# Layer 0 of a four-layer kernel: another order on TensorE, another split of one product, and a gate one step earlier

## The chip, the cores and the metric

The kernel runs on one core of one Trainium2 chip. The metric is the device time of one execution in microseconds, the median of several runs. Lower is better. A profile of one further execution shows where that time lies.

The core has five engines that the text names as the profile does: PE is TensorE (matrix products), PEld its weight loads, DVE is VectorE, ACT is ScalarE, POOL is GpSimd, and SP is SyncE, which issues the transfers. Each works through its own queue in order and waits where an operand or a buffer is not there yet.

## The reference, cut to what matters

The input has two images of 128 channels and 64 x 64 places. Four layers follow one another. Only layer 0 is touched: four selective scans over each image (row order, row order reversed, column order, column order reversed), fused and added to the input.

```python
xz = x @ W_in.T
xh, z = jnp.split(xz, 2, axis=-1)
...
xc = lax.conv_general_dilated(xc, conv_w, (1,), 'VALID', ..., feature_group_count=d_inner)
xc = xc + conv_b[None, :, None]
xh = jax.nn.silu(xc).transpose(0, 2, 1)
x_dbl = xh @ W_xp.T
dt = x_dbl[..., :dt_rank]
Bm = x_dbl[..., dt_rank:dt_rank + N]
Cm = x_dbl[..., dt_rank + N:]
dt = jax.nn.softplus(dt @ W_dt.T + b_dt)
A = -jnp.exp(A_log)
dA = jnp.exp(dt[..., None] * A)
dBu = dt[..., None] * Bm[:, :, None, :] * xh[..., None]

def step(h, inp):
    dA_t, dBu_t = inp
    h = dA_t * h + dBu_t
    return (h, h)
...
y = jnp.einsum('lbdn,bln->bld', hs, Cm)
y = y + xh * Dp
y = y * jax.nn.silu(z)
return y @ W_out.T
```

There are 256 inner channels with 16 states each, so 4096 scans of 4096 places for each order and image. Layer 1 and 2 are attentions, layer 3 is another scan.

## The kernel before, in words

Layer 0 is cut into 64 chunks: 2 images, 2 orders, forward and reversed, and 8 pieces of 512 places. Each chunk has 16 steps. A step handles two blocks of 128 rows (a row is one channel with one state), so the tiles are 128 x 1024. `gq` (line 154) says which states (`g`) and channels (`q`) step `u` has.

For step `u` the work is this. `s_dbu` (L336, GpSimd) makes dt x u x B. `s_da` (L349, ScalarE) makes exp(dt A) in two halves, into one of two PSUM buffers. `s_fix` (L361, L364, ScalarE) adds the state of the chunk before to the first place. `s_scan` (L380, VectorE) runs the recurrence. `s_hst` (L385, ScalarE) saves the last state. `s_hc` multiplies the scan's result by C: on VectorE (L392) with C spread over the rows by TensorE in PSUM, or on GpSimd (L390) with C brought by a transfer. Which steps go to GpSimd is `POOL_HC`. `s_pc` (L369, TensorE) makes that spread for a pair of steps; it has two PSUM buffers. `s_y` (L403, TensorE) sums the products over the states into the one PSUM buffer `y`. `y0` (L396) opens that buffer with the skip term. `yg_` (L410, VectorE) multiplies by the gate, `po_x` and `po` (L420, L425, TensorE) add the input to the projection, and `xo` (L430, L432, ScalarE) writes the image back. The buffers are few: three for `dbu`, three for `h`, four for `hc`, one for `y`, and one for `misc`, the PSUM tile that all other products of TensorE share in turn.

While a chunk `c` runs, pieces of its neighbours run between its steps: the end of the chunk before (`old`), the input work of the next (`new`) and of the one after (`nxt`), and in 12 chunks the normalisation of a later piece of the image. The dictionaries `M`, `A`, `V`, `G` say in which step TensorE, ScalarE, VectorE and GpSimd take such a piece. The pieces that the prediction uses are `pd` (L273, TensorE: dt, B, C before the bias), `xd_` (L278, ScalarE: with the bias), `pt` (L293, TensorE: the dt projection), `abs_`, `e_exp`, `e_ln` (L300, L303, L306, ScalarE: the softplus), `dt_` (L312, VectorE), `dtu_` (L320, GpSimd), `px` and `x_` (L238, L243), `pz` and `z_` (L247, L253). `pd` of the next chunk but one stands in step 15, and `xd_` of that same chunk in step 0 of the following chunk.

The order is written out by hand, under a manual schedule: the order in which the program calls these methods in a step is the order in each engine's queue. In a step it is: `s_dbu` of two steps ahead, the scan, a piece of VectorE, the product of the step before, a piece of GpSimd; then on ScalarE `s_da` and `s_fix` of the next step, the state, and ScalarE's pieces; then on TensorE the spread of C in odd steps, `y0`, the sums, and TensorE's piece; then the gate and the issues of transfers. The sums of a pair come two steps after a product on VectorE and three after one on GpSimd (`pairs`).

Of the kernel before, what the change touches and what calls it, by code (L numbers as in the profile page):

```python
# [16 lines left out]
T = 512  # L17
NCH = L // T
NS = 16
POOL_HC = (1, 5, 9, 11, 14)  # L20
GROUPS_C = (0, 2, 1, 3)
NHC, NH, NDBU = 4, 3, 3
ND = 73
# [33 lines left out]
def conv_seq_kernel(ctx: ExitStack, tc: tile.TileContext, a: dict, out: bass.AP):  # L57
    nc = tc.nc
    mm = nc.tensor.matmul
# [4 lines left out]
    def gt(shape, name, pool=None, **kw):  # L64
        return (pool or gp).tile(shape, F32, tag=name, name=name, **kw)
# [28 lines left out]
    with ExitStack() as c0:  # L94
# [6 lines left out]
        def misc(shape=(P, T)):  # L101
            return ps.tile(list(shape), F32, tag="misc", name="misc")
# [24 lines left out]
        wof = gt([P, 2, 4, P], "wof", wp)  # L127
# [88 lines left out]
        class Chunk:  # L216
# [170 lines left out]
            def s_hc(self, u):  # L387
                t = self.hc[u] = wt("hc", NHC)
                if u in POOL_HC:
                    nc.gpsimd.tensor_mul(t, self.h[u], _bc(self.cs[gq(u)[0]], 1, [P, 2, T]))  # L390
# [18 lines left out]
                    self.yg = wt("dt", 1)  # L409
                nc.vector.tensor_mul(self.yg[:, i, :], self.sz[:, i, :], self.y[i])  # L410

            def po_x(self):
                self.pp = p = misc()
                if self.order:
                    xo = x[:, self.b, :].rearrange("p (h w) -> p w h", w=W)
                    xo = xo[:, self.ci * 8 : self.ci * 8 + 8, :]
                    p = p.rearrange("p (w h) -> p w h", h=H)
                else:
                    xo = x[:, self.b, self.t0 : self.t0 + T]
                mm(p, lhsT=ident, rhs=xo, start=True, stop=False, skip_group_check=True)  # L420
                self.xo_ = xo, p

            def po(self):
                for i in range(2):
                    mm(self.pp, lhsT=wof[:, i, 2 * self.order + self.rev, :], rhs=self.yg[:, i, :],  # L425
                       start=False, stop=(i == 1), skip_group_check=True)

            def xo(self):
# [17 lines left out]
        for u in range(0, 16, 2):  # L446
            pairs.setdefault(max(m + (3 if m in POOL_HC else 2) for m in (u, u + 1)), []).append(u)

        with tc.manual_schedule():
            def norm(j):  # L450
                n = Norm0(0, j)
                for f in (n.center, n.sub, n.square, n.var, n.keep, n.ln, n.exp, n.rows, n.scale,
                          n.mul, n.affine):
                    f()

            for j in range(3):
                norm(j)
            c, c1 = chunks[:2]
            for i in range(2):
                c.px(i)  # L460
                c.x_(i)
            c.xsilu()
            c.pd()
            c.xd_()
            for i in range(2):
                c.pt(i)
                c.abs_(i)
            c.e_exp()
            c.e_ln()
            for i in range(2):  # L470
                c.pt(i)
                c.dt_(i)
                c.dtu_(i)
            c.spread("dts", 0)
            c.states(0, 0)
            c.spread("dus", 0)
            for g in range(1, 4):
                c.states(0, g)
            for g in GROUPS_C:
                c.states(1, g)  # L480
            c.spread("dts", 1)
            c.spread("dus", 1)
            for i in range(2):
                c.pz(i)
                c.z_(i)
            c.s_pc(0)
            c.s_dbu(0)
            c.s_dbu(1)
            c.s_da(0)
            c.s_fix(0)  # L490
            norm(3)
            for i in range(2):
                c1.px(i)
                c1.x_(i)
            c1.xsilu()
            c1.pd()
            old = None
            for k, c in enumerate(chunks):
                new, nxt = (chunks[k + i] if k + i < nk else None for i in (1, 2))
                ln, lp = norms.get(k), norms.get(k - 1)  # L500

                def at(u):
                    return (c, u) if 0 <= u < 16 else ((old, u + 16) if u < 0 else (new, u - 16))

                A, V, M, G = {}, {}, {}, {}
                if old is not None:
                    M[2], M[3], A[4] = old.po_x, old.po, (old.xo,)
                if c.rev:  # L510
                    A[4] = (*A[4], c.zload)
                else:
                    A[8] = (c.zsilu,)
                if new is not None:
                    A[0] = (new.xd_,)
                    M[0], A[1] = lambda: new.pt(0), (lambda: new.abs_(0),)
                    M[1], A[2] = lambda: new.pt(1), (lambda: new.abs_(1), new.e_exp)
                    A[3] = (new.e_ln,)
                    M[4], V[5] = lambda: new.pt(0), lambda: new.dt_(0)
                    M[5], V[6] = lambda: new.pt(1), lambda: new.dt_(1)  # L520
                    G[7], G[8] = lambda: new.dtu_(0), lambda: new.dtu_(1)
                    if not new.rev:
                        M[6], A[7] = lambda: new.pz(0), (lambda: new.z_(0),)
                        M[13], A[14] = lambda: new.pz(1), (lambda: new.z_(1),)
                if nxt is not None:
                    M[8], A[9] = lambda: nxt.px(0), (lambda: nxt.x_(0),)
                    M[10], A[12] = lambda: nxt.px(1), (lambda: nxt.x_(1),)
                    A[13] = (nxt.xsilu,)
                    M[15] = nxt.pd
                if lp is not None:  # L530
                    A[3] = (*A[3], lp.ln, lp.exp)
                    A[6] = (lp.rows,)
                    M[7], V[8] = lp.scale, lp.mul
                    A[10] = (lp.affine,)
                if ln is not None:
                    M[12], V[13] = ln.center, ln.sub
                    A[14] = (*A.get(14, ()), ln.square)
                    M[14], A[15] = ln.var, (ln.keep,)
                if k in turns:
                    A[11] = (lambda: turn(turns[k]),)  # L540

                for s in range(16):
                    (c1, u1), (c2, u2), (cp, up) = at(s + 1), at(s + 2), at(s - 1)

                    if c2 is not None:
                        c2.s_dbu(u2)
                    c.s_scan(s)
                    if s in V:
                        V[s]()
                    if cp is not None:  # L550
                        cp.s_hc(up)
                    if s in G:
                        G[s]()

                    if c1 is not None:
                        c1.s_da(u1)
                        c1.s_fix(u1)
                    if cp is not None:
                        cp.s_hst(up)
                    for f in A.get(s, ()):  # L560
                        f()

                    if s % 2 and s < 15:
                        c.s_pc(s + 1)
                    elif s == 15 and new is not None:
                        new.s_pc(0)
                    if s in (4, 11):
                        c.y0(s // 11)
                    for cy, e in ((c, s), (old, s + 16)):
                        for u in pairs.get(e, ()) if cy is not None else ():  # L570
                            cy.s_y(u)
                            cy.s_y(u + 1)
                    if s in M:
                        M[s]()

                    if s == 2 and old is not None:
                        old.yg_(1)
                    if s == 10:
                        c.yg_(0)

                    if new is not None:
                        if s in (7, 14):
                            new.spread("dts", s // 14)
                        if s in (9, 13):
                            new.spread("dus", s // 13)
                        if s in (8, 10, 12, 14):
                            new.states(0, s // 2 - 4)
                        if s in (11, 12, 13, 15):
                            new.states(1, GROUPS_C[{11: 0, 12: 1, 13: 2, 15: 3}[s]])
                old = c  # L590
            c.s_hc(15)
            for e in (16, 17):
                for u in pairs.get(e, ()):
                    c.s_y(u)
                    c.s_y(u + 1)
            c.yg_(1)
            c.po_x()
            c.po()
            c.xo()

# [11 lines left out]
    with ExitStack() as c1:  # L612
# [296 lines left out]
        for n, j in enumerate(jobs):  # L909
# [10 lines left out]
            if jobs[n - 1].layer == 1:  # L920
                for ci in range(NCH):
                    c = Conv(jobs[n - 1].b, ci)
# [62 lines left out]
    with ExitStack() as c3:  # L985
# [276 lines left out]
        with tc.manual_schedule():  # L1262
            c = chunks[0]
# [13 lines left out]
            for s in range(-1, len(steps) + 3):  # L1277
# [3 lines left out]
                old = chunks[ci - 1] if ci > 0 else None  # L1281
# [209 lines left out]
```

## Time and profile before

| | us |
|---|---|
| median of 3 runs | 6928.74 |
| lowest and highest run | 6912.35, 6931.16 |
| the profiled execution's own time | 6921.35 |
| its span, first to last instruction | 6919.6 |
| layer 0 in it, from the first scan to the end of its last pieces | 108 to 3588 |
| granted clock of TensorE, whole span | 0.863 |

The page gives the busy time of each engine over the whole span: PE 6036.7 (87%), DVE 5525.2 (80%), POOL 5366.3 (78%), ACT 4467.5 (65%). Slices of the page are 173 us each; layer 0 fills the first 20 and a part of the 21st. In a timeline row the first number is the start, the second the time, then engine, line, operation, the tile written and the tiles read; brackets hold the idle time before the row and what ended it. In the waits the columns are the total, how often, and the longest.

### The profile page before, as it was taken

Reading aid. Unit: us, or ns where it says so; the run is one execution under the profiler, and the core shown is the slowest. Engines: PE = TensorE matmul, PEld = TensorE weight load, DVE = VectorE, ACT = ScalarE, POOL = GpSimd, SP = SyncE. Lnnn points to the kernel's source line nnn. Section 1 sums busy time; section 2 is a strip of 40 time slices with the busy share of each in tenths; the row PEclk is TensorE's granted clock in tenths of the full one; section 3 lists DMA queues with packets and bytes.
Section 4 is the critical chain, followed back from the end, with each engine's and each line's share of the span. In section 5 each row is a group of like instructions: output and inputs, shape, how many; then the busy total and the mean of one; then the engine's idle time right before and its main releaser. Section 6 shows DMA issues by size and latency. Waiting matters only on the chain. (4 is left out here: it accounts for less than half of the span.)

```text
span 6919.6 us, 67264 instructions
## 1 busy us (share of the span) xinstructions
PE 6036.7 (87%) x20656; PEld 2806.4 (41%) x20656; DVE 5525.2 (80%) x4494; ACT 4467.5 (65%) x7688; POOL 5366.3 (78%) x2487
## 2 busy tenths in 40 slices
PE   6888888888888888888868999999999997988888
PEld 1222222222222222222217887788788884222222
DVE  3899999999999999999975665566566675887777
ACT  4887778877788777887755665455456554434342
POOL 3899999899999999999975665555556666777776
PEclk8777788787777777777779999999999998889888
DMA  3555565556555655656540000000000001222222
GB/s 111 135 147 148 145 153 139 138 148 152 138 152 149 153 145 145 154 148 151 141 136 7 3 5 1 1 1 1 1 1 13 1 1 54 69 75 75 86 75 67
DMA packets 352652, 616.51 MB, mean 89 GB/s; under 512 B 72473, under 2 KB 74786, under 8 KB 351906
## 3 DMA queue, kind: packets, MB, share of 16 engines
q1 hardware_dynamic: 351552, 610.44, 34.1%
q8 instruction: 162, 2.65, 0.2%
q14 instruction: 200, 1.64, 0.1%
q10 hardware_dynamic: 738, 1.78, 0.1%
HBM read 496.45 MB, written 115.47 MB: 88 GB/s over the span
## 5 line engine op out<-in xcount | busy, mean ns | idle before, releaser
L336 POOL TENSOR_TENSOR dbu<-dus,bs 128x1024 f32<-128x1024 f32 x1024 | 2401.8, 2365 | 216.9 <-DVE h L380 192.6
L380 DVE TENSOR_TENSOR_SCAN h<-da,hst,dbu 128x1024 f32<-128x1024 f32 x896 | 2092.6, 2343 | 120.6 <-ACT dbu L364 120.1
L349 ACT ACTIVATE da<-dts,aneg 128x512 f32<-128x512 f32 (+1 forms) x2048 | 1410.8, 689 | 412.9 <-DVE h L380 373.2
L833 POOL TENSOR_TENSOR sum<-sum,sc 128x1024 f32<-128x1024 f32 x384 | 906.8, 2361 | 495.2 <-ACT sc L828 491.5
L795 ACT COPY sc<-s 128x512 f32<-128x512 f32 x1024 | 597.9, 585 | 867.8 <-PE s L790 753.6
L790 PE MATMUL s<-q,k 128*128 128x256 f32 x4096 | 1058.0, 382 | 11.6 <-ACT q L776 8.4
L802 DVE TENSOR_TENSOR mx<-mx,s 128x512 f32<-128x512 f32 x896 | 610.1, 681 | 569.6 <-ACT sc L795 568.5
L845 PE MATMUL av<-sc,v 128*128 128x256 f32 x4096 | 1049.7, 379 | 2.3 <-ACT sc L828 2.3
L369 PE MATMUL pc<-xd,sel 16*128 16x512 f32 x1024 | 723.1, 792 | 241.4 <-DVE hc L392 241.1
L392 DVE TENSOR_TENSOR hc<-h,pc 128x1024 f32<-128x1024 f32 x704 | 843.2, 1198 | 0.1
L790 PEld LDWEIGHTS s<-q,k 128*128 128x128 f32 x4096 | 781.2, 192 | 146.2 <-issue 36.6
L845 PEld LDWEIGHTS av<-sc,v 128*128 128x128 f32 x4096 | 769.1, 190 | 103.1 <-ACT sc L828 3.7
L403 PE MATMUL y<-hc,cst 128*32 128x512 f32 x4096 | 725.2, 711 | 60.5 <-POOL hc L390 57.7
L390 POOL TENSOR_TENSOR hc<-h,cs 128x1024 f32<-128x1024 f32 x320 | 757.0, 2366 | 1.3 <-issue 1.3
L1160 POOL TENSOR_TENSOR A<-A,D 128x1024 f32<-128x1024 f32 x224 | 526.8, 2368 | 225.3 <-DVE D L1165 201.4
L825 DVE TENSOR_TENSOR sc<-sc,pm 128x1024 f32<-128x1024 f32 x512 | 620.9, 1214 | 0.9 <-PE pm L821 0.9
L828 ACT ACTIVATE sc<-sc 128x1024 f32<-128x1024 f32 x512 | 541.9, 1059 | 8.6 <-DVE sc L825 8.1
L1153 ACT ACTIVATE A<-dtr,aneg 128x1024 f32<-128x1024 f32 (+1 forms) x256 | 245.8, 1030 | 376.3 <-PE y L1185 369.9
L369 PEld LDWEIGHTS pc<-xd,sel 16*128 16x128 f32 x1024 | 180.7, 219 | 622.1 <-DVE hc L392 271.6
L1171 DVE TENSOR_TENSOR A<-A,q 128x1024 f32<-128x1024 f32 (+1 forms) x256 | 276.8, 1081 | 148.1 <-PE q L1137 147.6
L1137 PE MATMUL q<-xs,lb 32*128 32x512 f32 x896 | 332.2, 713 | 69.5 <-DVE D L1147 64.1
L293 PE MATMUL misc<-xd,w_dt 9*128 9x512 f32 x512 | 304.2, 675 | 63.0 <-ACT xd L278 50.7
(210 smaller groups left out, 8065.0 us busy)
## 6 DMA issues: line engine op xcount, KB each, us to landing
dts<-ddt SPq DMA_DIRECT2D x512, 256.0 KB, 5.2
dus<-ddu SPq DMA_DIRECT2D x512, 256.0 KB, 4.9
bs<-rows SPq DMA_DIRECT2D x1024, 64.0 KB, 4.7
cs<-rows SPq DMA_DIRECT2D x1024, 64.0 KB, 3.2
ddt<-dt SPq DMA_DIRECT2D x128, 256.0 KB, 2.0
ddu<-dtu SPq DMA_DIRECT2D x128, 256.0 KB, 2.3
dtr<-ddt SPq DMA_DIRECT2D x448, 64.0 KB, 1.9
rx<-ddx SPq DMA_DIRECT2D x448, 64.0 KB, 1.9
```

The lines of the kernel that those rows point to most:

```text
L336: nc.gpsimd.tensor_mul(t, self.dus[q], _bc(self.bs[g], 1, [P, 2, T]))
L349: act(t[:, i, sl], self.dts[q][:, i, sl], AF.Exp, scale=an[:, g, 2 * q + i : 2 * q + i + 1])
L369: mm(t, lhsT=sel[32:48, 4 * g : 4 * g + 4, :].rearrange("p n d -> p (n d)"), rhs=self.xd[32:48, :], start=True, stop=True)
L380: nc.vector.tensor_tensor_scan(ho, ai, bi, init, ALU.mult, ALU.add)
L390: nc.gpsimd.tensor_mul(t, self.h[u], _bc(self.cs[gq(u)[0]], 1, [P, 2, T]))
L392: nc.vector.tensor_mul(t, self.h[u], _bc(self.pc[u // 2], 1, [P, 2, T]))
L403: mm(self.y[q // 2][r : r + 32, :], lhsT=sum4, rhs=self.hc[u][:, i, :], start=False, stop=(u % 8 >= 6), skip_group_check=True)
L790: mm(p[:, o, :], lhsT=j.k[m // 8][:, m % 8 * P : m % 8 * P + P], rhs=self.q, start=True, stop=True)
L802: nc.vector.tensor_max(self.mx, self.s[0][:, 0:2, :] if u == 1 else self.mx, self.p[u])
L825: nc.vector.tensor_sub(s, s, _bc(self.pm[:, :], 1, [P, 4, NQ]))
L833: nc.gpsimd.tensor_add(self.sum, self.s[0] if w == 1 else self.sum, self.s[w])
L845: mm(self.av, lhsT=self.job.v[m // 8][:, m % 8, :], rhs=self.s[u // 2][:, m % 4, :], start=(m == 0), stop=(m == 31))
```

## The change

Four things are done, all in layer 0. On TensorE the spread of C (`s_pc`) is called after the sums and the piece of a step, where it was called before them. `POOL_HC` has step 0 in place of step 1, so GpSimd multiplies the result of step 0 by C and VectorE that of step 1; with this the sums of the first pair move from step 4 to step 3. The second half of the gate of the chunk before (`old.yg_(1)`) is called in step 1 and not in step 2, and `y0(0)` in step 3 and not in step 4. `po_x` becomes a part of `po`, and the whole stands in step 2, where before its first product stood in step 2 and the other two in step 3.

```diff
-POOL_HC = (1, 5, 9, 11, 14)
+POOL_HC = (0, 5, 9, 11, 14)
...
-            def po_x(self):
-                self.pp = p = misc()
+            def po(self):
+                p = misc()
...
+                self.xo_ = xo, p
                 mm(p, lhsT=ident, rhs=xo, start=True, stop=False, skip_group_check=True)
-                self.xo_ = xo, p
-
-            def po(self):
+                if self.order:
+                    p = p.rearrange("p w h -> p (w h)")
                 for i in range(2):
-                    mm(self.pp, lhsT=wof[:, i, 2 * self.order + self.rev, :], rhs=self.yg[:, i, :],
+                    mm(p, lhsT=wof[:, i, 2 * self.order + self.rev, :], rhs=self.yg[:, i, :],
                        start=False, stop=(i == 1), skip_group_check=True)
...
-                    M[2], M[3], A[4] = old.po_x, old.po, (old.xo,)
+                    M[2], A[4] = old.po, (old.xo,)
...
-                    if s % 2 and s < 15:
-                        c.s_pc(s + 1)
-                    elif s == 15 and new is not None:
-                        new.s_pc(0)
-                    if s in (4, 11):
+                    if s in (3, 11):
                         c.y0(s // 11)
                     for cy, e in ((c, s), (old, s + 16)):
                         for u in pairs.get(e, ()) if cy is not None else ():
...
                     if s in M:
                         M[s]()
-
-                    if s == 2 and old is not None:
+                    if s % 2 and s < 15:
+                        c.s_pc(s + 1)
+                    elif s == 15 and new is not None:
+                        new.s_pc(0)
+
+                    if s == 1 and old is not None:
                         old.yg_(1)
...
             c.yg_(1)
-            c.po_x()
             c.po()
             c.xo()
```

## The prediction

> **What bounds the kernel now.** I read the page's busy shares and its slices first: PE shows 87%, but layer 0 (the first 20 slices) is where the change lies, and there DVE and POOL stand at 9 in every slice. So I cut the span at the end of the last scan. TensorE's granted clock, in tenths by slice:
>
> ```profile
> PEclk8777788787777777777779999999999998889888
> ```
>
> The first 20 digits lie mostly at 7 and 8. The table by stretches has layer 0 as one row:
>
> ```profile
> 108.00:3588.00 3480.00, 2921.11 (x7785) 785.30 (x7786) 3276.66 (x2007) 2749.36 (x5242) 3270.85 (x1468) 0.78 0.58 145
> ```
>
> The columns are the stretch, its length, then busy time of PE, weight loads, DVE, ACT, POOL, then the granted clock. DVE works 3276.7 of 3480.0 us, POOL 3270.9. Each idles about 205 us, 3.2 us in each of the 64 chunks. The change adds and removes no VectorE or GpSimd work, so it can win only from these 205 us (3.0% of the kernel); it can lose without limit. Who ends the waits:
>
> ```profile
> DVE h L380 <- ACT dbu L364: 120.1, 158, 2.9
> DVE dt L312 <- PE pc L369: 19.5, 34, 1.2
> DVE dt L410 <- issue: 16.0, 16, 1.7
> DVE dt L410 <- PE y L403: 13.2, 13, 1.2
> ACT xd L278 <- PE misc L273: 131.7, 60, 5.1
> ```
>
> Columns: total us, times, longest. VectorE's scan waits mostly for ScalarE's fix of the carried state (L364), which stands behind the whole ScalarE queue; and ScalarE itself stood 131.7 us (2.2 us a chunk) before `xd_`, waiting for TensorE's `pd`. The timeline of one reverse chunk (its first scan starts at 1556.05) shows the link:
>
> ```profile
> 1553.20 2.07 PE L369 MATMUL pc<-xd,sel 16*128 16x512 f32 x2 [2.64 <-DVE hc L392]
> 1555.20 1.94 PE L403 MATMUL y<-hc,cst 128*32 128x512 f32 x8
> 1557.07 3.69 PE L273 MATMUL misc<-xs,m 128*73 128x512 f32 x4
> 1560.80 0.68 ACT L278 ACTIVATE xd<-misc,vec 73x512 f32<-73x512 f32 x1 [2.43 <-PE misc L273]
> 1561.53 0.69 PE L293 MATMUL misc<-xd,w_dt 9*128 9x512 f32 x1 [0.77 <-ACT xd L278]
> 1561.54 0.69 PE L369 MATMUL pc<-xd,sel 16*128 16x512 f32 x1
> 1562.59 1.07 PE L403 MATMUL y<-hc,cst 128*32 128x512 f32 x8
> ...
> 1574.07 2.35 DVE L380 TENSOR_TENSOR_SCAN h<-da,hst,dbu 128x1024 f32<-128x1024 f32 x1 [1.27 <-ACT dbu L364]
> ```
>
> pc, sums and `pd` follow each other at half clock; `xd_` waits 2.43; ScalarE then runs without a gap from 1560.80 until scan(5), which is 1.27 late. In the next chunk the same three ran partly at full clock, `xd_` came 1.9 us sooner after its first scan, and scan(5) did not wait. Chunk lengths differ accordingly:
>
> ```profile
> 1556.05:1610.15 54.10, 45.82 (x127) 12.06 (x120) 51.07 (x32) 41.10 (x82) 51.31 (x24) 0.78 0.59 148
> 1610.15:1661.87 51.72, 41.14 (x114) 10.76 (x116) 50.94 (x33) 41.27 (x82) 50.97 (x24) 0.83 0.60 153
> 2038.62:2093.56 54.94, 47.32 (x126) 12.71 (x122) 51.30 (x32) 46.45 (x90) 51.23 (x24) 0.75 0.57 145
> 1221.29:1279.30 58.01, 49.45 (x135) 14.22 (x134) 52.60 (x34) 48.28 (x98) 51.45 (x24) 0.79 0.55 139
> ```
>
> Rows 1 and 2: reverse chunks (32 of 64, idle about 1.95 us in the mean of the timeline). Row 3: a forward chunk (19, idle 3.1). Row 4: a forward chunk that also normalises (12, idle 5.4). POOL's 51.0 to 51.4 us of work lies close below every length: a chunk cannot get much under 51.5.
>
> **The change, part by part.** In each part I say who gains.
>
> *The spread of C behind sums and pieces.* No instruction is added. In step 15 `pd` no longer stands behind pc: it starts 2.07 us sooner in the row above (1.1 at full clock). `xd_` then starts when ScalarE is ready: after the state copy that ends at 1558.37, or when `pd` ends (1553.20 + 1.94 + 3.69 = 1558.83). So 1558.85 for 1560.80, 1.95 sooner. In normalising chunks (the row of `xd_` at 1285.54 waits 3.95) it is 2.0 sooner, because `misc` is free (L185 ends at 1279.50). In step 9 the sums of 6 and 7 come 1.1 us sooner, and the gate of step 10 (33 us idle in all, 0.9 in a forward chunk) stops waiting. But scan(11) then meets da(11), behind `x_(0)`, which waits for the end of `px(0)`; that did not move. In the forward chunk da(11)'s fix ends 0.4 before the present scan(11), so 0.4 of the 0.9 is kept, and in normalising chunks nothing: there the norm's piece now goes ahead of pc(8), waits for `z_(0)`, and pushes `px(0)` back by about 0.6. What now queues behind pieces: pc(2) behind pt(1), which waits for `abs_`; pc(4) behind the sums of 0 and 1; pc(6) behind pt(1), which waits for VectorE's `dt_(0)`; pc(8) and pc(14) behind norm and z pieces. Their readers on VectorE come one or two steps later (hc(2) some 4 us after pc(2) would end), so I cost these at nothing; without that cover each would cost up to its 1.1 to 2.1 us.
>
> *The gate of the old chunk in step 1, `po` in one piece in step 2.* Same VectorE work (0.67 us), one step sooner. Cost: the sums of 14 and 15 must end by the end of scan(1), 1559.40 + 2.34 = 1561.74; before, they had until scan(2), 3.7 us later. Their chain is `xd_`, pt(0), sums. From `xd_` at 1558.85: 0.68 + 0.05, pt(0) 1.12, sums 1.07, 0.1 to be seen: 1561.9, a stall of 0.15 at full clock. At half clock pt(0) 2.0 and sums 1.94 make it 1563.6, a stall of 1.9. Behind the waiting gate stand scan(2) and hc(1) on VectorE; for scan(2) wait da(4) on ScalarE and dbu(5) on GpSimd. In forward chunks `xd_` can start 2.15 after the first scan: stall 0 to 1.3. In normalising ones it starts 4.2 after: 1.6 to 3.3. I take 0.5, 0.35 and 2.1, near the full-clock end, because in the two reverse chunks the half clock ends between 2.6 and 6.0 us after the first scan, and pt(0) and sums would run from 3.5 on.
>
> [...] The rows show the pair pt(0) and pc at 1561.53 and 1561.54, both done after 1.12 us: [...] Now pc(0) of the new chunk stands ahead of pt(0) and the two start about 0.7 us apart; [...] if they run in turn, pt(0) is up to 2.0 later and the reverse chunk stalls up to 3. No row shows them staggered; [...] from 1553.20 to 1560.76 PE had no gap, and still the half clock lasted until about 1562. By that row the stall is 1.9. My 0.5 lies nearer to the fast chunk.
>
> *GpSimd takes product 0, not 1.* 2.37 us of POOL and 1.20 of DVE each trade one step. POOL runs dbu(2), dbu(3), dbu(4) back to back (7.00 from 1557.81), then hc(1). Now hc(0) stands between dbu(3) and dbu(4): dbu(4) ends at 1567.2 instead of 1564.8. fix(4) on ScalarE, which would come to it at 1566.35, waits 0.8 in reverse chunks; behind it stand the Ln with two table loads and da(5). From fix(4) to scan(5) it is 5.89 (1568.18 to 1574.07), so scan(5) is at 1573.1: 1.0 sooner than in the slow chunk, but 0.55 to 0.85 later than in the fast one. Forward chunks have 1 us more lead on POOL and pay about nothing. hc(0) must free the buffer that scan(3) writes: 0.9 to 1.4 us to spare.
>
> **The sum**, per chunk. Reverse: scan(5) gains 1.0 or loses 0.7 in turn (+0.15), the dt wait (0.86 in slow ones, later `po` no longer in its way) +0.2, stall beyond what the wait at scan(5) hides -0.3: about 0; x32 = 0. Forward: scan(5) is now bound by VectorE alone, 0.6 sooner after the stall, plus 0.4 at scan(11): 1.0; x19 = 19. Normalising: 1.5 at scan(5) with a stall of 1.7, 1.1 with my 2.1, less 0.25 at scan(11): 0.85; x12 = 10. Together 29 us. The other layers, the DMA issues (none is moved) and chunk 0 are left as they are. The profiled execution took 6921.35 us (span 6919.6, 1.75 around it), so 6892; the median of the runs, 6928.74, lies 7.4 higher and gives 6900. I say 6895.
>
> **Rivals.**
> *Everything is hidden* (0.13): stall 0, fix(4) not late. Reverse chunks go to 51.9 (0.9 each), forward gain 1.9, normalising 2.6: 29 + 36 + 31 = 96, so 6830. For it: the fast chunk's 51.72. Against: POOL's own 51.0 to 51.4 leaves no lead there.
> *No difference* (0.18, within 0.3%, 6908 to 6950, which is about what a measurement can tell): half-clock stalls eat the 29 us; 6925.
> *Slower* (0.37): the gate in step 1 stalls because pt(0) runs behind pc(0) at half clock. Stalls 3.0, 2.4, 3.5: reverse +1.9, forward +0.75, normalising +0.35, 61 + 14 + 4 = 79, so 7000; with half the chunks at full clock about 6960. I put it at 6970. It decides from about 0.5 us more stall per chunk than I took (29/63 eats the gain), 0.8 for slower by 0.3%. For it: the clock row of 0.78. Against: the fast chunk's sums ended in time for exactly this gate.
>
> **How the numbers follow.** Likeliest: a small gain, 6895 (own range 6865 to 6915), chance 0.32 that it is over 0.3%, and the part of it that is less goes to "no difference". Faster: 0.32 + 0.13 = 0.45; same 0.18; slower 0.37. Range: 6820 below the full gain's 6830, and 6990 above, near the full stall's 7000; about 0.1 is left outside on each side.
>
> **What would show it.** Right: the wait of `xd_` for `pd` falls from 131.7 to below 60 us; waits of the gate (L410 before) at step 10 vanish and new ones at step 1 stay under 50 us in all; scan waits for L364 fall from 120 to about 70; reverse chunks all near 52.8. ScalarE's fix waits for GpSimd's dbu(4) some 20 to 30 us, where it was 5.2. Wrong: the gate waits for PE more than 100 us, or the granted clock in layer 0 moves by more than 0.02 from 0.78.

## The result

The changed kernel takes 6866.9 us (median of 6 runs, 6855.92 to 6880.17); the kernel before, on the same chip, 6920.51 (median of 6, 6906.10 to 6931.16). The ratio is 0.9924, 95% interval 0.9906 to 0.9941: 54 us or 0.76% faster. The forecast was 6895, with 6865 to 6915 as the range of its likeliest case. The direction was right, but the gain is nearly twice the 29 us of its sum. The runs below show that the move in step 15, where the forecast put most of the gain, pays only together with a part that it counted at nothing, and that two of the other parts cost time.

The profiled executions are 59 us apart: 6921.35 before, 6862.33 after (span 6860.5). Layer 0, from the first scan to the last, went from 3474.8 to 3426.5, which is 48.3. The other 10.8 lie outside that stretch, where the program is the same. Over all kernels below what lies outside took 3429 to 3451 us with nothing changed in it, so I compare layer 0 where I compare traces.

TensorE's granted clock by slice, and layer 0 as one row (stretch, length, then busy time of PE, weight loads, DVE, ACT, POOL, granted clock, DMA share, GB/s):

```profile
PEclk8777777778777777777769999999999998988898
```

```profile
108.00:3540.00 3432.00, 2908.18 (x7782) 804.08 (x7780) 3272.33 (x2006) 2755.18 (x5242) 3268.35 (x1468) 0.77 0.59 147
```

VectorE and GpSimd have the same work as before (3272 and 3268 us); what went is idle time, some 205 us before and 160 now. The mean clock is 0.77 where it was 0.78, so it gave nothing. Some of the waits, by what ended each (total us, times, longest):

```profile
ACT xs L243 <- PE misc L238: 81.1, 43, 4.4
DVE h L380 <- ACT dbu L364: 74.6, 130, 1.4
ACT dbu L364 <- POOL dbu L336: 39.3, 48, 2.2
DVE dt L410 <- PE y L403: 34.9, 34, 1.9
ACT xd L278 <- PE misc L273: 28.8, 22, 2.5
DVE dt L410 <- issue: 22.4, 10, 2.6
```

`xd_`'s wait for `pd` fell from 131.7 to 28.8 us, the scan's wait for the fix (L364) from 120.1 to 74.6. Two waits are new: 34.9 us of the gate for the sums (before 13.2, in another step), and 39.3 us of the fix for GpSimd's `dbu` (before 5.2). The reverse chunk that was shown of before, in the timeline of after (its first scan is at 1541.32):

```profile
1538.47 1.92 PE L403 MATMUL y<-hc,cst 128*32 128x512 f32 x4 [1.45 <-DVE hc L392]
...
1540.33 3.36 PE L273 MATMUL misc<-xs,m 128*73 128x512 f32 x4
...
1543.61 1.12 PE L369 MATMUL pc<-xd,sel 16*128 16x512 f32 x2
1543.72 0.68 ACT L278 ACTIVATE xd<-misc,vec 73x512 f32<-73x512 f32 x1
...
1544.46 1.12 PE L293 MATMUL misc<-xd,w_dt 9*128 9x512 f32 x2
...
1545.51 1.07 PE L403 MATMUL y<-hc,cst 128*32 128x512 f32 x8
...
1546.64 0.69 PE L293 MATMUL misc<-xd,w_dt 9*128 9x512 f32 x1
...
1546.65 0.69 PE L369 MATMUL pc<-xd,sel 16*128 16x512 f32 x1
...
1546.94 0.66 DVE L410 TENSOR_TENSOR dt<-sz,y 128x512 f32<-128x512 f32 x1
...
1552.38 0.39 ACT L364 ACTIVATE dbu<-hst,dbu,df 128x1 f32<-128x1 f32 x1 [0.63 <-POOL dbu L336]
...
1558.28 2.35 DVE L380 TENSOR_TENSOR_SCAN h<-da,hst,dbu 128x1024 f32<-128x1024 f32 x1 [0.56 <-ACT dbu L364]
```

Sums, `pd`, pc is now the order; `xd_` starts 2.40 after the first scan, where it started 4.75 after. pt(0) and the sums follow, and the gate at 1546.94 comes before scan(2). Then the fix of step 4 waits 0.63 for `dbu`, and scan(5), 16.96 after the first scan (18.02 before), still waits 0.56. The same four chunks as before, by stretch:

```profile
1208.53:1266.52 57.99, 49.21 (x138) 14.86 (x137) 52.39 (x34) 48.24 (x98) 51.37 (x24) 0.76 0.54 135
1541.32:1593.39 52.07, 43.42 (x120) 11.69 (x119) 50.88 (x33) 41.33 (x82) 50.67 (x24) 0.79 0.61 150
1593.39:1646.87 53.48, 45.03 (x122) 12.38 (x120) 50.98 (x32) 41.27 (x82) 51.73 (x24) 0.80 0.61 151
2015.18:2068.69 53.51, 45.79 (x120) 12.39 (x121) 51.23 (x32) 46.37 (x90) 51.19 (x24) 0.75 0.59 149
```

The reverse pair went from 54.10 and 51.72 to 52.07 and 53.48, the forward chunk from 54.94 to 53.51, the normalising chunk from 58.01 to 57.99.

### The profile page after: what moved, and what is told of

Same layout as the page of the kernel before. It is cut to its first block, busy times and chain, and to the rows that moved or that the text cites. A ratio compares the mean times of both kernels' runs of the same rounds, so it can differ in the third digit from the quotient of the medians.

```text
span 6860.5 us, 67328 instructions
## 1 busy us (share of the span) xinstructions
PE 6008.4 (88%) x20656; PEld 2820.0 (41%) x20656; DVE 5521.4 (80%) x4494; ACT 4472.9 (65%) x7688; POOL 5358.9 (78%) x2487
## 5 line engine op out<-in xcount | busy, mean ns | idle before, releaser
L380 DVE TENSOR_TENSOR_SCAN h<-da,hst,dbu 128x1024 f32<-128x1024 f32 x896 | 2090.9, 2341 | 77.3 <-ACT dbu L364 74.6
L403 PE MATMUL y<-hc,cst 128*32 128x512 f32 x4096 | 811.6, 759 | 177.9 <-DVE hc L392 103.6
L392 DVE TENSOR_TENSOR hc<-h,pc 128x1024 f32<-128x1024 f32 x704 | 841.2, 1195 | 0.1
L293 PE MATMUL misc<-xd,w_dt 9*128 9x512 f32 x512 | 394.9, 860 | 157.3 <-ACT x L432 81.6
L403 PEld LDWEIGHTS y<-hc,cst 128*32 128x32 f32 x4096 | 105.7, 117 | 743.2 <-issue 334.8
```

Of the source, the lines that this page charges most:

```text
L380: nc.vector.tensor_tensor_scan(ho, ai, bi, init, ALU.mult, ALU.add)
L392: nc.vector.tensor_mul(t, self.h[u], _bc(self.pc[u // 2], 1, [P, 2, T]))
L403: mm(self.y[q // 2][r : r + 32, :], lhsT=sum4, rhs=self.hc[u][:, i, :], start=False, stop=(u % 8 >= 6), skip_group_check=True)
```

## The experiments

All kernels were timed beside the kernel before, whose median in the four groups of runs was 6920.51, 6917.21, 6916.45 and 6915.36; so the ratios can be set beside each other. "Order" is the place of the spread of C behind sums and piece. The last columns are from the traces: layer 0 from first to last scan, and the mean length of normalising (N), forward (F) and reverse (R) chunks, without the first and the last chunk.

| kernel | median us | ratio to before, 95% | layer 0 | N | F | R |
|---|---|---|---|---|---|---|
| before | 6920.51 | 1 | 3474.8 | 57.57 | 54.35 | 52.81 |
| after | 6866.90 | 0.9924, 0.9906 to 0.9941 | 3426.5 | 57.08 | 52.65 | 52.55 |
| e1 order in step 15 only | 6944.98 | 1.0040, 1.0028 to 1.0053 | 3508.8 | 55.98 | 54.95 | 54.20 |
| e2 after, without the order | 6926.27 | 1.0008, 1.0000 to 1.0017 | 3481.5 | 57.77 | 54.34 | 52.95 |
| e3 after, gate and `po` as before | 6873.47 | 0.9934, 0.9920 to 0.9948 | 3423.7 | 56.78 | 52.63 | 52.57 |
| e4 after, product 1 on GpSimd | 6863.83 | 0.9917, 0.9903 to 0.9930 | 3418.2 | 57.35 | 53.03 | 51.96 |
| e5 order alone, not in step 7 | **6798.41** | 0.9833, 0.9820 to 0.9847 | 3362.1 | 54.57 | 52.61 | 51.46 |
| e6 order in steps 15, 1, 3 only | 6822.03 | 0.9866, 0.9853 to 0.9880 | 3380.2 | 55.49 | 52.85 | 51.52 |
| e7 after, old order in step 15 | 6922.62 | 1.0015, 1.0006 to 1.0024 | 3485.4 | 59.30 | 53.47 | 53.04 |
| e8 e1 with a longer spread | 6984.90 | 1.0101, 1.0087 to 1.0115 | 3537.8 | 58.44 | 54.61 | 54.38 |
| e9 after, old order in step 7 | 6850.27 | 0.9905, 0.9890 to 0.9920 | 3407.4 | 55.09 | 52.67 | 52.69 |
| e10 e9, product 1 on GpSimd | 6822.67 | 0.9868, 0.9854 to 0.9881 | 3385.5 | 54.82 | 52.83 | 51.99 |
| e11 order alone, all steps | 6828.59 | 0.9876, 0.9861 to 0.9890 | 3388.4 | 56.96 | 52.50 | 51.48 |

### e1: only `pd` ahead of pc(0)

The forecast puts most of the gain in step 15: `pd` out of the shadow of pc(0). So that alone, in the kernel before.

```diff
                     if s % 2 and s < 15:
                         c.s_pc(s + 1)
-                    elif s == 15 and new is not None:
-                        new.s_pc(0)
...
                         M[s]()
+                    if s == 15 and new is not None:
+                        new.s_pc(0)
```

> The kernel before, with one edit: in step 15 the spread of C for the new chunk goes behind pd. Theory A (the gain of the change comes from pd leaving the shadow of that one spread, so that xd_ starts sooner, and the gate in step 1 and the product 0 on GpSimd give a part of it back): the wait of xd_ for pd falls from 131.7 to about 30 us, VectorE's waits for ScalarE's fix from 120 to about 70, the dt waits from 19.8 to about 5, no stall of the gate in step 1, the 33 us of the gate in step 10 stay: 60 us under the kernel before (6845 to 6875), as fast as the changed kernel or a little faster. Theory B (the gain comes from the gate, the projection and the sums being sooner): within 10 us of the kernel before.

Measured: 6944.98, 28 us slower than before, ratio 1.0040 (1.0028 to 1.0053). The wait of `xd_` did fall as forecast, and new ones took its place:

```profile
DVE h L380 <- ACT dbu L364: 129.6, 137, 1.9
ACT e L300 <- PE misc L293: 102.1, 76, 2.3
DVE dt L312 <- PE pc L369: 48.7, 48, 1.8
ACT xd L278 <- PE misc L273: 23.7, 13, 3.7
```

`xd_` waits 23.7 us and not 131.7, but `abs_` (L300), the next piece of the softplus on ScalarE, waits 102.1 for pt(1) (L293), and `dt_` (L312, VectorE, step 5) waits 48.7 where it waited 19.5. One reverse chunk of e1, first scan at 1660.48, in the timeline:

```profile
1660.49 1.12 PE L369 MATMUL pc<-xd,sel 16*128 16x512 f32 x2
...
1662.70 0.68 ACT L278 ACTIVATE xd<-misc,vec 73x512 f32<-73x512 f32 x1
...
1663.43 1.22 PE L293 MATMUL misc<-xd,w_dt 9*128 9x512 f32 x1 [1.82 <-ACT xd L278]
...
1663.97 1.22 PE L369 MATMUL pc<-xd,sel 16*128 16x512 f32 x1
...
1664.44 1.06 PE L293 MATMUL misc<-xd,w_dt 9*128 9x512 f32 x1
...
1664.98 1.06 PE L369 MATMUL pc<-xd,sel 16*128 16x512 f32 x1
...
1665.97 1.94 PE L403 MATMUL y<-hc,cst 128*32 128x512 f32 x8
...
1667.84 2.07 PE L293 MATMUL misc<-xd,w_dt 9*128 9x512 f32 x2
...
1669.94 0.60 ACT L300 ACTIVATE e<-misc 128x512 f32<-128x512 f32 x1 [1.93 <-PE misc L293]
...
1678.76 2.35 DVE L380 TENSOR_TENSOR_SCAN h<-da,hst,dbu 128x1024 f32<-128x1024 f32 x1 [1.88 <-ACT dbu L364]
```

`xd_` is 2.22 after the first scan, as in after. But pc(2), still called before the sums, stands between pt(0) and the sums of 14 and 15: from the start of pt(0) to the end of the sums it is 4.48 us (1663.43 to 1667.91), where the chunk of after took 2.12 (1544.46 to 1546.58). pc(2) uses the buffer that VectorE's product 15 of the old chunk reads, and that product ends 3.4 us after the first scan (the mean of reverse and of forward chunks, in before, e1, e6 and after alike). In before, pt(0) starts later than that and pc(2) runs beside it; in e1 pt(0) starts at 2.9, so pc(2) ends after it and holds up the sums. A part of the 4.48 is the clock: in the trace it is halved from 1662.9 to 1680.0, so pt(0), sums and pt(1) all ran at half clock, which in the chunk of after had ended at 1543.2. pt(1) ends 9.43 after the first scan, `abs_` had waited 1.93, and behind it on ScalarE stand the second half of the softplus, da(5) and the fix, and scan(5) is 1.88 late. So the early `pd` alone is worth nothing; whether the spreads of steps 1 and 3 are the reason is what e6 asks.

### e2: the change without its order

```diff
+                    if s % 2 and s < 15:
+                        c.s_pc(s + 1)
+                    elif s == 15 and new is not None:
+                        new.s_pc(0)
                     if s in (3, 11):
...
                         M[s]()
-                    if s % 2 and s < 15:
-                        c.s_pc(s + 1)
-                    elif s == 15 and new is not None:
-                        new.s_pc(0)
```

> The changed kernel, with the spread of C back ahead of sums and pieces; the gate in step 1, the projection in step 2 and product 0 on GpSimd are kept. Theory A: xd_ is as late as before (wait about 130 us), so the sums of 14 and 15 come after the end of scan(1) and the gate stalls in step 1 by 1 us in reverse, 1.7 in forward and 3.7 in normalising chunks, 32 + 32 + 44 = 108 us, of which some 60 take the place of the waits at scan(2) and scan(5): slower than the kernel before by 20 to 70 us. Theory B: at most 20 us slower than the changed kernel.

Measured: 6926.27, 1.0008 (1.0000 to 1.0017), hardly to be told from before, and 59 us above after. By its waits:

```profile
ACT xd L278 <- PE misc L273: 141.9, 62, 4.0
DVE dt L410 <- PE y L403: 122.6, 72, 3.5
DVE h L380 <- ACT dbu L364: 47.1, 92, 1.8
```

The gate's stall came as large as expected, 109.8 us in step 1, but the loss did not. Waits that VectorE would have had later gave way to it: at scan(5) 3.4 us are left of 57.8, at `dt_` 0.5 of 19.8, at scan(2) none of 22.8. Here the stall of VectorE let ScalarE and GpSimd catch up, so it may not be added to the waits behind it. Gate, `po` and product without the order gain nothing.

### e3 and e4: one of the other parts undone

e3 puts the gate back to step 2 and `po` in two pieces; e4 gives GpSimd product 1 again. In both `y0(0)` stays in step 3.

```diff
-                    M[2], A[4] = old.po, (old.xo,)
+                    M[2], M[3], A[4] = old.po_x, old.po, (old.xo,)
...
-                    if s == 1 and old is not None:
+                    if s == 2 and old is not None:
                         old.yg_(1)
```

```diff
-POOL_HC = (0, 5, 9, 11, 14)
+POOL_HC = (1, 5, 9, 11, 14)
```

> The changed kernel, with the gate of the old chunk back in step 2 and the projection back in two parts (steps 2 and 3). Theory A: the 34 us of stalls of the gate in step 1 go; a part of them comes back as waits at scan(5), where ScalarE's fix is behind: 10 to 25 us faster than the changed kernel. Theory B: slower than the changed kernel by 20 us or more, since the gate's place is what gained.

> The changed kernel, with product 1 on GpSimd and product 0 on VectorE as before. Theory A: dbu(4) is no longer behind a product, ScalarE's fix waits for dbu fall from 39 to about 10 us, and the waits at scan(5) in reverse chunks by about 0.5 us each: 5 to 15 us faster than the changed kernel. Theory B: steps 1 and 2 of VectorE become uneven (hc and gate both in step 1), 20 us slower than the changed kernel.

Measured: e3 6873.47 (0.9934, 0.9920 to 0.9948), e4 6863.83 (0.9917, 0.9903 to 0.9930). Neither can be told from after's 0.9924 (0.9906 to 0.9941); both were expected to gain. The waits of e3, then those of e4:

```profile
DVE h L380 <- ACT dbu L364: 106.8, 169, 1.4
ACT dbu L364 <- POOL dbu L336: 40.0, 48, 2.7
```

```profile
DVE h L380 <- ACT dbu L364: 89.8, 161, 1.3
ACT dbu L364 <- POOL dbu L336: 11.7, 19, 1.4
```

In e3 the 34.0 us of gate stall are gone and the scans' wait for the fix is 32 us longer (106.8 for 74.6): what the gate gave back is lost at scan(5) and, in normalising chunks, at scan(2).

In e4 the fix no longer waits for `dbu` in step 4 (11.7 us in all for 39.3), and the reverse chunks did gain what was expected, 0.59 us each (52.55 to 51.96), 18 us together. The forward and normalising chunks gave 10 of them back (0.38 and 0.27 each), and scan(5) idles 41.2 us for 25.8. The trace shows why: VectorE now has product 0 and the gate ahead of scan(2), which starts 7.32 after the first scan in reverse chunks, where it starts at 6.45 in after and at 6.72 in e11 below, which has neither edit. ScalarE's da(4) waits for that scan, 0.40 us in the mean of 24 of these chunks, and ScalarE then works without a pause to the fix of step 5. So scan(5) comes at 16.9 in e4, between the 16.5 of e11 and the 17.4 of after.

### e5 and e11: the order alone

e11 is the kernel before with the spread last in all odd steps; e5 leaves it first in step 7, where the forecast had pointed to a cost in normalising chunks.

```diff
-                    if s % 2 and s < 15:
-                        c.s_pc(s + 1)
-                    elif s == 15 and new is not None:
-                        new.s_pc(0)
+                    if s == 7:
+                        c.s_pc(8)
...
                         M[s]()
+                    if s % 2 and s < 15 and s != 7:
+                        c.s_pc(s + 1)
+                    elif s == 15 and new is not None:
+                        new.s_pc(0)
```

(e11 has neither the two lines for step 7 nor `and s != 7`.)

> The kernel before, with the order on TensorE alone: the spread of C behind sums and pieces in every odd step but step 7 (where the norm's piece would have to wait for it the other way round). Product 1 on GpSimd, the gate in step 2, the projection in two parts, as before. Theory C (the order of the spreads is the whole gain, but not by the one in step 15 alone: those of steps 1 and 3 lengthen the chain pt, abs_, po, y0, sums, pt in the half-clock stretch): 6845 to 6875, as the changed kernel. Theory D (order, gate and product gain only together): above 6900.

> Experiment five with the spread of step 7 behind the norm's piece as well; nothing else differs. Theory F: the normalising chunks go back from 54.6 to 58.0, 12 x 3.4 = 41 us slower than experiment five: about 6840. Theory G: within 10 us of experiment five.

Measured: e5 **6798.41**, 0.9833 (0.9820 to 0.9847), 118 us under before and 68 under after: the best kernel of all, some 50 us better than theory C expected. e11 6828.59, 0.9876 (0.9861 to 0.9890), 87 us under before and 38 under after, and 30 over e5, where theory F expected 41. So the order is more than the whole gain, and gate, `po`, `y0` and product 0 together take 38 us of it back. The waits of e5:

```profile
DVE h L380 <- ACT dbu L364: 71.7, 137, 1.3
ACT dbu L364 <- POOL dbu L336: 15.6, 26, 1.5
ACT xd L278 <- PE misc L273: 22.8, 25, 2.4
```

No row of the gate is left that counts, and the fix waits 15.6 us for `dbu`. Its reverse chunks take 51.46 in the mean; GpSimd's own work in one of them is 51.1:

```profile
1604.17:1655.62 51.45, 45.53 (x120) 11.80 (x119) 50.82 (x32) 41.24 (x82) 51.12 (x24) 0.73 0.63 154
```

### e6: steps 1 and 3 added to e1

```diff
-                    if s % 2 and s < 15:
+                    if s % 2 and 3 < s < 15:
                         c.s_pc(s + 1)
...
                         M[s]()
+                    if s in (1, 3):
+                        c.s_pc(s + 1)
                     if s == 15 and new is not None:
```

> Experiment one and, besides, the spreads of steps 1 and 3 behind the sums and pieces; those of steps 5 to 13 stay first. Theory C: the wait of abs_ for pt falls from 102 us to below 40 and the reverse chunks leave their 54.6 us: 6850 to 6890. If the clock's phase alone decides (theory E: the half clock falls on the chain because TensorE has a gap between the spread of step 15 and pt(0)): as slow as experiment one, 6930 or more.

Measured: 6822.03, 0.9866 (0.9853 to 0.9880), 123 us under e1 and better than expected. Worked out from the traces, the means over 30 reverse chunks, in us after the chunk's first scan:

| | `xd_` starts | pt(0) ends | sums of 14, 15 end | pt(1) ends | second `abs_` starts | scan(5) starts |
|---|---|---|---|---|---|---|
| before | 3.75 | 5.60 | 6.76 | 8.19 | 8.45 | 17.22 |
| e1 | 2.15 | 4.77 | 7.28 | 9.25 | 9.30 | 18.05 |
| e6 | 2.44 | 4.31 | 5.44 | 7.24 | 7.62 | 16.46 |
| e11 | 2.42 | 4.28 | 5.40 | 7.05 | 7.60 | 16.48 |
| after | 2.32 | 4.32 | 5.56 | 7.40 | 7.83 | 17.39 |

e1 has the earliest `xd_` and the latest scan(5). With pc(2) and pc(4) behind the pieces the sums end 1.84 sooner and scan(5) comes 1.59 sooner. The last row is what after gives back: its chain up to `abs_` is that of e11 within 0.23, and scan(5) is 0.91 later.

VectorE's idle time shows where the 128.6 us between the layers 0 of e1 and e6 lie: at scan(5) it fell from 94.6 to 29.1, and the 48.7 at `dt_` are gone. The second is pc(4)'s part. It stood ahead of `po`, so `po`, the sums of 0 and 1 and the pt(0) that `dt_` reads came later: in reverse chunks that pt(0) starts at 20.5 in e1 and at 17.3 in e6.

Is it the order or the clock? In reverse chunks both changed: the sums of 14 and 15 ran at half clock in 29 of the 30 in e1 and in 5 in e6, pt(0) in 25 and in 1. From the start of `xd_` to the end of these sums e6 is 2.1 us shorter. Of that, 0.7 lie between pt(0) and the sums, where pc(2) stood, and 1.5 in pt(0) and the sums themselves, which ran faster. In forward chunks the clock was much the same (sums at half clock in 17 of 19 in e1 and in 14 in e6, pt(0) in 9 and in 11), and there the sums start 1.03 us sooner, scan(5) 0.97, and the chunk is 2.10 shorter. So in forward chunks the order gains without help of the clock; in reverse chunks the clock went with the order, and no run separates the two.

### e7: the change with the old order in step 15

```diff
+                    if s == 15 and new is not None:
+                        new.s_pc(0)
                     if s in (3, 11):
...
                         c.s_pc(s + 1)
-                    elif s == 15 and new is not None:
-                        new.s_pc(0)
```

> The changed kernel, with the spread of C back at the head of step 15 alone. Theory A in its mended form (pd sooner is needed, though not enough): xd_ waits about 130 us again, the gate stalls in step 1 for some 100 us, and the time is that of the kernel before, 6910 to 6950. Theory C: at most 15 us above the changed kernel.

Measured: 6922.62, 1.0015 (1.0006 to 1.0024), as expected (the profiled execution was the longest of its ten, 6938.35). Its waits are those of before and those of the gate in step 1:

```profile
ACT xd L278 <- PE misc L273: 149.2, 62, 5.7
DVE dt L410 <- PE y L403: 114.7, 60, 5.2
```

e2 differs from e7 by the order in steps 1 to 13, and is 4 us slower. So without step 15 the rest of the order gains next to nothing here: forward chunks are 0.87 us shorter than in e2, normalising ones 1.53 longer. e7 has the lowest granted clock of all kernels (0.85 over the span, 0.86 in the others), but pt(0) and the sums of 14 and 15 ran at full clock in all 62 chunks between its first and its last, so the clock does not make this chain late. Step 15 is needed and, by e1, not enough: the order pays when the whole chain `pd`, pt(0), sums, pt(1) is free of spreads. One case was not run: the order without step 15 and with the gate in step 2.

### e8: does a busier TensorE keep the clock up?

In e1 TensorE is idle 1.82 us ahead of pt(0) and then runs at half clock. A rival to "pc(2) and pc(4) are in the way" was that the gap itself costs, through the clock. e8 fills the gap: it is e1 with the first spread of each chunk computed three times into the same tile, which adds work and leaves the output as it is.

```diff
+                for _ in range(1 if u else 3):
-                mm(t, lhsT=sel[32:48, 4 * g : 4 * g + 4, :].rearrange("p n d -> p (n d)"),
-                   rhs=self.xd[32:48, :], start=True, stop=True)
+                    mm(t, lhsT=sel[32:48, 4 * g : 4 * g + 4, :].rearrange("p n d -> p (n d)"),
+                       rhs=self.xd[32:48, :], start=True, stop=True)
```

> Experiment one with more work: the first spread of each chunk is computed three times, the same values into the same tile, in the gap of 1.8 us that TensorE has there before pt(0). Theory E (the gap lets the clock fall to half for the chain that follows): the reverse chunks fall from 54.6 to 53 or below, 30 us or more under experiment one, though TensorE does 2 x 0.9 us more per chunk. Theory C or any theory of plain throughput: no faster than experiment one, and up to 60 us slower where the extra products run at half clock.

Measured: 6984.90, 1.0101 (1.0087 to 1.0115), 40 us slower than e1. Scan(5) idles 95.4 us (94.6 in e1), and 23.6 us at scan(4) are new. In the trace pt(0) now runs at half clock in 1 of 30 reverse chunks, where in e1 it was 25. So pt(0) did get the full clock, as theory E has it. But the added products and pc(2) behind them end later, the sums run at half clock in 28 of 30 all the same and end at 7.96 (7.28 in e1), and scan(5) comes at 18.73 (18.05). Filling the gap in this way is no cure, and it doesn't show that the clock plays no part in e1's loss. A higher mean clock is not what makes the fast kernels fast: over the reverse chunks it is 0.79 in before, 0.78 in e1, and 0.77 in e5 and e11. What sets e1 apart from e6 and e11 is that the half clock falls on this chain: from the start of `xd_` to the end of the sums it takes 5.13 us in e1, 3.00 in e6 and 2.98 in e11.

### e9 and e10: step 7, and then product 1

e9 is after with the spread of step 7 first again; e10 is e9 with product 1 on GpSimd.

```diff
+                    if s == 7:
+                        c.s_pc(8)
                     if s in M:
                         M[s]()
-                    if s % 2 and s < 15:
+                    if s % 2 and s < 15 and s != 7:
                         c.s_pc(s + 1)
```

> The changed kernel, with the spread of C of step 7 ahead of the norm's piece again. Theory F (the 12 normalising chunks gained nothing because there the norm's piece waits for z_(0) at the head of TensorE's queue, which sends px(0) and the sums for the gate of step 10 back): those chunks fall from 58.0 to about 54.6, the waits of the gate in step 10 from 25 to about 1 us, 35 to 45 us faster than the changed kernel: 6820 to 6835. Theory G (the gate in step 1 and product 0 are what separates it from experiment five): at most 10 us faster than the changed kernel.

> The changed kernel, with the spread of step 7 first and product 1 on GpSimd; what then separates it from experiment five is the gate in step 1, the projection in one part and y0 in step 3. Theory F: ScalarE's fix waits for dbu no longer in step 3, reverse chunks 52.0 instead of 52.6: 15 to 25 us faster than experiment nine, 5 to 20 us slower than experiment five (6800 to 6820). Theory G: within 10 us of experiment four (6864).

Measured: e9 6850.27, 0.9905 (0.9890 to 0.9920), a median 17 us under after, less than half of what was expected, and with intervals that overlap. e10 6822.67, 0.9868 (0.9854 to 0.9881), 28 us under e9, a little more than expected. The mechanism of step 7 is in the normalising chunks; one each of e11, e9 and e5, by stretch:

```profile
1196.25:1254.24 57.99, 49.53 (x138) 14.79 (x135) 52.56 (x33) 48.13 (x98) 51.30 (x24) 0.76 0.55 138
```

```profile
1193.23:1247.90 54.67, 46.77 (x138) 13.59 (x134) 52.40 (x33) 48.23 (x98) 51.18 (x24) 0.81 0.58 145
```

```profile
1181.66:1236.31 54.65, 47.06 (x142) 13.47 (x134) 52.38 (x33) 48.16 (x98) 51.27 (x24) 0.81 0.59 146
```

With pc(8) last such a chunk takes 58.0, with pc(8) first 54.7, at a higher granted clock (0.81 for 0.76). In step 10 the gate idles 25.1 us in after and 2.3 in e9. In the normalising chunk of after from 1208.53 the norm's piece (L201) waits for `z_(0)`, pc(8) and the sums of 4 and 5 follow, then px(0), for the most part at half clock, and only then the sums of 6 and 7, for which the gate waits:

```profile
1235.82 0.59 ACT L253 COPY sz<-misc 128x512 f32<-128x512 f32 x1 [0.51 <-PE misc L247]
...
1236.46 2.07 PE L201 MATMUL misc<-sq,ones 128*128 128x512 f32 x2 [0.68 <-ACT sz L253]
...
1242.33 5.64 PE L238 MATMUL misc<-xnt,wk 128*128 128x512 f32 x8
...
1247.89 1.06 PE L403 MATMUL y<-hc,cst 128*32 128x512 f32 x8
...
1249.08 0.69 DVE L410 TENSOR_TENSOR dt<-sz,y 128x512 f32<-128x512 f32 x1 [2.46 <-issue]
```

In the chunk of e9 pc(8) runs while `z_(0)` is still being written. There px(0) ends 36.13 after the first scan, here 39.44. Of the 3.31 it starts 1.77 sooner, which is pc(8)'s time, and takes 1.54 less, which is the clock's (in the chunk of after it stood at half from 1229.19 to 1246.26). Between e5 and e11, which differ in step 7 alone, the 12 normalising chunks give 12 x 2.39 = 28.7 us; the medians are 30 apart. Between after and e9 they give 12 x 1.99 = 24, and the medians are 17 apart.

The other parts are dear once step 7 is right: from e9 to e10 product 1 gives 28 us, and from e10 to e5 gate, `po` and `y0` as before give 24.

## Why the prediction was right, and where not

**`pd` sooner in step 15, 1.95 to 2.0 per chunk.** Right in size in the chunk it was read from (2.40 for 4.75 us after the first scan; 1.4 in the mean of the reverse chunks), and `xd_` waits 28.8 us, under the 60 named as the sign. Wrong as the whole cause: e1 has it and is 28 us slower, e7 lacks it and is no faster than before.

**"I cost these at nothing"** is where the forecast's picture of the cause fails. It was about the spreads that now queue behind pieces, pc(2) and pc(4) foremost. I asked only what a later spread may cost its reader, and that was indeed nothing: among VectorE's waits in layer 0 of after none is one of its product (L392) for pc. I did not ask what stood behind those spreads. Behind pc(2) stood the sums of 14 and 15 and pt(1), which are on the path to scan(5); behind pc(4) stood `po`, the sums of 0 and 1 and the pt(0) that `dt_` reads. From e1 to e6 this term measures 123 us. The forecast's own chain (`xd_`, pt(0), sums) has no spread in it, so it counted on a part of this gain without naming it, and put it down to step 15.

**Forward chunks, 1.0 each.** They gained 1.70 (19 x 1.70 = 32 us), and here the sum was too small. By VectorE's idle time per chunk, the gate's wait in step 10 fell from 0.87 to 0.02 and only 0.11 of it came back at scan(11), where the forecast kept 0.4 of 0.9. scan(5) less the new stall gave 0.4 for 0.6. And 0.3 at `dt_`, with 0.2 at scan(15), were not in the sum.

**Reverse chunks, 0.** They gained 0.26 (32 x 0.26 = 8 us), about as much as the wait at `dt_` fell (0.44 to 0.14; the forecast had 0.2 for it).

**The stall of the gate in step 1**, forecast at 0.5, 0.35 and 2.1 per chunk (48 us in all), measured 34.0. The half-clock rival with 3.0 per reverse chunk did not come: pc(0) and pt(0), staggered, ran side by side. In the lines of after above pc(0) runs from 1543.61 to 1544.73 and pt(0) starts at 1544.46, 0.06 behind `xd_`. In all 62 chunks between the first and the last pt(0) starts 0.05 after the end of `xd_`, in 29 of them while pc(0) still runs. So here pc(0) did not hold pt(0) back, as the forecast had assumed without a row that showed it.

**Product 0 delays fix(4) by 0.8 in reverse chunks.** Right: fix(4) waits 0.78 there in the mean, 23 us over all chunks, within the 20 to 30 named. The rest of the 39.3 lies at other steps, where e11 has 14.8 too. What the forecast and the expectation of e4 missed is that this cost and the gate's do not add up. Against e11 a reverse chunk is 1.09 longer with product 0 alone (e3), 0.48 with the gate in step 1 alone (e4), and 1.07 with both (after); these three also have `y0(0)` in step 3. Product 0 holds up fix(4), the gate holds up da(4) by way of scan(2), both push back scan(5), and the longer delay counts. So undoing the gate alone gains nothing there, undoing product 0 alone 0.59 a chunk, and both together 38 us over the kernel.

**Normalising chunks, 0.85 each.** They gained 0.49 (6 us in all), and the late ones nothing (58.01 to 57.99). scan(5) came 1.48 sooner, as forecast (1.1 to 1.5). The failed term is step 7: "pushes `px(0)` back by about 0.6", counted as -0.25. It costs about 2 to 2.4 per chunk (e9, e5 against e11), most of it in the late chunks as some 2.45 us before the gate of step 10, a wait that the forecast had seen vanish everywhere. In the chunk shown nearly half of it comes by the clock.

**Signs.** Scan waits for the fix "to about 70": 74.6. Gate waits in step 1 under 50: 34.0. Reverse chunks near 52.8: 52.55. The clock within 0.02 of 0.78: 0.77. Gate waits in step 10 "vanish": they did in forward and reverse chunks (22.1 us before, 0.4 after), but in normalising ones they grew from 11.3 to 24.7.

**The sum** by chunks: 32 + 8 + 6 = 46 us, with 48.3 measured in layer 0, for 19 + 0 + 10 = 29. Some terms were too small and some too large, the cause was in part another, and that the measured time still fell into the likeliest case is in part luck.

## What to carry to other kernels

When a piece of work is moved behind others in a queue, cost both sides: what its reader loses, and what everything that it stood in front of gains, down to the next wait on the bounding path. Take a bundle of changes apart: here one part alone was worth 118 us, with one step of it left as it was, while the bundle gave 54. And where two changes feed the same late instruction, their costs need not add up: undo both before concluding that neither matters.

## What the hardware showed that I had not expected

Normalising chunks do not vary smoothly. The 4th, 20th and 21st chunk take 57.9 to 58.1 us in before, after and e11, and 54.6 to 54.8 in e5, e9 and e10 (though e9 has two near them at 55.7 and 56.5); the reverse chunks of e1 stand at 54.6 seven times in a row. The rows by stretch have a granted clock of 0.79 (before) and 0.76 (after, e11) at 58.0 us, and of 0.81 (e5, e9) at 54.7. The 181 stretches of half clock in layer 0 of after last 3.4 us (45 of them), 6.8 (43), 10.2 (59), 13.7 (21), 17.1 (11), and once each 20.5 and 27.3. The two lengths of the chunks lie as far apart as the shortest of these, but that the one comes from the other is not shown: the reverse chunks of e5 and of e4 are just as regular at 51.45 and 52.05, and no run moved the clock alone.

No long pause went ahead of the half clock here. In the 6.8 us before each of these 181 stretches the longest pause of TensorE in the trace was 1.4 us in the median and 3.2 at most.
